# Two attention layers on one core: the softmax sums folded by adding DMAs and summed one block later

## The chip, the core and the metric

The kernel runs on one core of a Trainium2 chip. The metric is the device time of one execution in microseconds (us), as the median of several runs. Engine names are those of the profile: PE is the matmul engine (TensorE) and PEld its weight loads, DVE is VectorE, ACT is ScalarE, POOL is GpSimd, SP is the engine that issues most DMAs. A line such as L431 is line 431 of the kernel before. All arrays are float32.

## What is computed

Two layers, each with its own weights, on x of shape (16, 256, 32, 32), so 16 images of 256 channels and 1024 positions:

```
def layer(x, Wq, bq, Wk, bk, Wv, bv, rel_h, rel_w):      # 4 heads of d = 64 channels
    xf = group_norm(x).reshape(16, 256, 1024)             # 16 groups over the last axis
    q, k, v = (proj(W, b) for W, b in ((Wq, bq), (Wk, bk), (Wv, bv)))   # (16, 4, 64, 1024)
    sim  = einsum('bhdi,bhdj->bhij', q, k)
    qpos = einsum('hdi,bhdj->bhij', (rel_h + rel_w).reshape(4, 64, 1024), q)
    attn = softmax(sim + qpos, axis=-1)
    out  = einsum('bhdn,bhmn->bhdm', v, attn)
    return x + out.reshape(x.shape)
x = layer(x, *layer0); x = layer(x, *layer1)
```

The softmax needs, for each of the 1024 query positions of each head, the sum of 1024 exponentials. How these sums are formed is what the change is about. The kernel takes exp(s - 36) without a maximum, and a flag at the end says whether all sums were in a safe range.

## The kernel before

An image in one layer is a unit; there are 32 units, `u`. A unit has two pairs of heads (`pr`), and a pair of heads is worked in two halves of 512 queries (`half`). So there are 128 blocks, `n`, four to a unit (`b` = 0 to 3). A block with half 0 (n even) and the next one with half 1 (n odd) make a pair of blocks and share one pair of heads.

In a block, the keys come in eight tiles of 128 (`j` = 0 to 7). For each tile DVE first writes the position term into PSUM (`seed`, L338), PE adds q times k onto it (`scores`, L374: 8 instructions, four 64x64 quarters of the array in two passes), ACT takes the exponential into an SBUF tile p (L383), and DVE adds p to a running sum of 128 rows by 2 heads by 512 queries (`add_up` into `acc`, L392 for the first, L394 for the others). Then PE multiplies p by v (`attend`, L408), 128 instructions in two stretches of 64, `values_of_p(0)` and `values_of_p(1)`. Between these, PE already does the scores of tile 0 of the next block.

The partial sum `acc` still has 128 rows, one for each key modulo 128. At the end of an odd block `sums_of_p` (L431) sums the rows of both blocks of the pair with 8 products against a column of ones: 128 rows deep, 32 columns wide, 256 queries long, 16 instructions. ACT copies the values and the sums out of PSUM (`take_out`, L443 in an even block, L448 in an odd one), and SP spreads the sums over partitions into `den_all` (L459, four small DMAs for a pair). In the next block, which is even, `reciprocals` (L467 on DVE, then L470 and L473 on SP) brings 1/sum to all rows as `rden`, and `finish` (L484 and L485 on DVE, 128x1024 each) scales the output and adds bias and x; in layer 1 SP then stores it (L487).

Beside this, each block does two pieces of preparation for what comes next, `first` and `second`: projections of q, k and v (L257, L287) and the position term (L315). Even blocks have two full products there; odd blocks have one full product and the shorter position term. ACT also does the group norm of later units, spread over the blocks: `norm_sums` and `norm_squares` (L182), `norm_apply` (L237). Small products for the mean and the variance (L202, `pm`) stand in the odd blocks, between the two stretches of `values_of_p`.

The order of every engine is the order of the program: the schedule is written by hand, and each engine works off its own list. What couples them:

- Four double banks of PSUM take turns under the names `ring[0]` to `ring[3]`. In a block, the tiles 4 and 6 use the same one (`f1`), so the seed of tile 6 waits until ACT has read the scores of tile 4. Tiles 5, and 0 and 3 of the next block, use `f0`; tile 1 of the next block uses `f1` again, and so does `pm`.
- Scores of a tile come after its seed on DVE and after everything that stands before them on PE. PE does `scores` 1 to 3, `first(0)`, `scores` 4, `second(0)`, `first(1)` and so on.
- A product in two stretches writes the two PSUM banks with exchanged halves of the array. Before the second stretch, POOL sets a one-element `token` when the first is done (`word`, L158), and PE waits for the token. The token is POOL's only work in most blocks; once a unit POOL also takes a power for the norm (L226, L228).

The calls that order DVE's list in `block` before the change:

```
if half == 1: add_up(blocks[n - 1], 7)
seed(blk, 4, f1); add_up(blk, 1)
if half == 0: reciprocals(*before); add_up(blk, 2)
...
add_up(blk, 4); seed(after, 0, f0)
if before: finish(*before)          # even blocks
add_up(blk, 5)
if half == 1: add_up(blk, 6); add_up(blk, 7)
for j in range(1, 4): seed(after, j, ring[j % 3])
if half == 0: add_up(blk, 6)
```

Of the kernel before, what the change touches and what calls it, by code (L numbers as in the profile page):

```python
# [17 lines left out]
P = 128  # L18
# [34 lines left out]
def fast_path(ctx, tc, sh, x, layers, out, W, den_all, token, good, flag):  # L53
# [19 lines left out]

    nc = tc.nc
    B, C, H, N, CC, NT, NH, D, GT = (
        sh.B, sh.C, sh.H, sh.N, sh.CC, sh.NT, sh.NH, sh.D, sh.GT
# [9 lines left out]
    vpool = ctx.enter_context(tc.tile_pool(name="vpool", bufs=2))  # L88
    ppool = ctx.enter_context(tc.tile_pool(name="ppool", bufs=12))
    apool = ctx.enter_context(tc.tile_pool(name="apool", bufs=3))  # L90
    fpool = ctx.enter_context(tc.tile_pool(name="fpool", bufs=2))
    opool = ctx.enter_context(tc.tile_pool(name="opool", bufs=2))
    dpool = ctx.enter_context(tc.tile_pool(name="dpool", bufs=2, space=bass.MemoryType.DRAM))
# [324 lines left out]

    index, rdens = {}, {}

    def sums_of_p(two, po):

        R = P // 4
        for a in range(2):
            for x, blk in enumerate(two):
                for h in range(2):
                    r0 = (2 * x + h) * R  # L430
                    nc.tensor.matmul(  # L431
                        po[r0 : r0 + R, a, QUART:],
                        W.ones[:, :R],
                        accs[blk][:, h, a * QUART : (a + 1) * QUART],
                        start=True, stop=True, tile_position=(0, r0), skip_group_check=True,
                    )

    def take_out(blk, po):

        u, pr, half = blk  # L440
        if half == 0:
            outs[u, pr] = opool.tile([P, 3, HALF], F32, tag="od", name=f"od_{u}_{pr}")
            nc.scalar.copy(  # L443
                outs[u, pr][:, 0, :].rearrange("p (a n) -> p a n", a=2), po[:, :, :QUART]
            )
            return
        od = outs[u, pr]
        nc.scalar.copy(  # L448
            od[:, 1:3, :].rearrange("p z (a n) -> p z a n", a=2),
            po.rearrange("p a (z n) -> p z a n", z=2),  # L450
        )
        keep_sums(od, index[blk] - 1, 2)

    def keep_sums(od, n, count):
        R = P // 4
        for x in range(count):
            for h in range(2):
                r0 = (2 * x + h) * R
                nc.sync.dma_start(  # L459
                    den_all[h * D : (h + 1) * D, n + x, :], od[r0 : r0 + 1, 2, :]  # L460
                )
# [36 lines left out]

    def in_range(den, i):

        t = small.tile([P, den.shape[-1]], F32, tag=f"range{i}", name=f"range{i}")
        nc.vector.tensor_scalar(t, den, DEN_LO, None, ALU.is_ge)
        nc.vector.scalar_tensor_tensor(t, den, DEN_HI, t, ALU.is_le, ALU.mult)
        nc.vector.tensor_reduce(good[:, i : i + 1], t, AX.X, ALU.min)

    def sums_on_rows(acc, pd):

# [55 lines left out]
    def block(n):  # L563
        blk = blocks[n]
        u, b = divmod(n, BPU)
        half = blk[2]
        before = blocks[n - 2][:2] if half == 0 and n > 0 else None
        after = blocks[n + 1] if n + 1 < len(blocks) else None
        one, two = u + 1 < NU, u + 2 < NU

        pieces = u + 1 < NU or b < 2
        if u + 1 == NU and b == 1:
            widen(u, 1)
        f0, f1, f2, f3 = ring
        if not pieces:
            return block_without_pieces(n, half)

        if half == 1:
            add_up(blocks[n - 1], 7)
        for j in range(1, 4):  # L580
            scores(blk, j)
        if b == 3 and u + 3 < NU and units[u + 3][0] not in xt:
            load_x(units[u + 3][0])
        (first, first_out), (second, second_out) = prepare(u, b)
        first(0)
        if b == 0 and one:
            norm_apply(u + 1, range(0, 1))
        if b == 1 and two:
            norm_sums(u + 2, range(9, 11))
        seed(blk, 4, f1)  # L590
        scores(blk, 4)
        add_up(blk, 1)
        if half == 0:
            if before:
                reciprocals(*before)
            add_up(blk, 2)
        if b == 0 and one:
            norm_apply(u + 1, range(1, 5))
        if b == 1 and two:
            norm_sums(u + 2, range(11, 12))  # L600
        if b == 2 and two:
            norm_squares(u + 2, range(0, 5))
        second(0)
        if half == 1:
            second_out()
        first(1)
        first_out()
        seed(blk, 5, f0)
        scores(blk, 5)
        if half == 0:  # L610
            add_up(blk, 3)
            second(1)
            second_out()
        seed(blk, 6, f1)
        scores(blk, 6)
        if half == 0:
            ring[2:] = f3, f2
        seed(blk, 7, ring[2])
        scores(blk, 7)
        if half == 1:  # L620
            add_up(blk, 2)
            add_up(blk, 3)
        add_up(blk, 4)

        if after:
            seed(after, 0, f0)
        if before:
            finish(*before)
        if b == 0 and one:
            norm_apply(u + 1, range(5, 9))  # L630
        if b == 0 and two:
            norm_sums(u + 2, range(0, 2))
        if b == 1 and two:
            norm_sums(u + 2, range(12, G))
        if b == 1 and one:
            norm_apply(u + 1, range(9, 11))
        if b == 2 and two:
            norm_squares(u + 2, range(5, 11))
        po = psum2(ring[3], f"po_{n}")
        values_of_p = attend(blk, po)  # L640
        values_of_p(0)
        if two and half == 1:
            mean, mean_out = (norm_mean if b == 1 else norm_var)(u + 2, zeroed(f1, f"pm_{n}"))
            mean(0)
        if after:
            scores(after, 0)
        if two and half == 1:
            mean(1)
            values_of_p.word()
            mean_out()  # L650
        add_up(blk, 5)
        if half == 1:
            add_up(blk, 6)
            add_up(blk, 7)
        if after:
            for j in range(1, 4):
                seed(after, j, ring[j % 3])
        if half == 0:
            add_up(blk, 6)
        if b == 0 and two:  # L660
            norm_sums(u + 2, range(2, 9))
        if b == 1 and one:
            norm_apply(u + 1, range(11, G))
        if b == 2 and two:
            norm_squares(u + 2, range(11, G))
        values_of_p(1)
        if half == 1:
            sums_of_p(blocks[n - 1 : n + 1], po)
        take_out(blk, po)

    flatden = den_all.rearrange("p n e -> p (n e)")

    def block_without_pieces(n, half):

        blk = blocks[n]
        u, pr, _ = blk
        f0, f1, f2, f3 = ring
        if half == 1:
            add_up(blocks[n - 1], 7)
        for j in range(1, 4):  # L680
            scores(blk, j)
        if half == 1:
            po = pos[n - 1]
            sums_of_p(blocks[n - 1 : n], po)
            nc.scalar.copy(
                outs[u, pr][:D, 2, :].rearrange("p (a n) -> p a n", a=2), po[:D, :, QUART:]
            )
            keep_sums(outs[u, pr], n - 1, 1)
        add_up(blk, 1)
        seed(blk, 7, f2)  # L690
        add_up(blk, 2)
        reciprocals(*(blocks[n - 2][:2] if half == 0 else (u, pr, 1)))
        add_up(blk, 3)
        for j, tag in ((4, f1), (5, f0), (6, f1)):
            scores(blk, j, tag)
        scores(blk, 7)
        add_up(blk, 4)
        if half == 0:
# [11 lines left out]
            seed(blocks[n + 1], 3, f0)  # L710
        add_up(blk, 6)
        if half == 0:
            finish(*blocks[n - 2][:2])
            in_range(flatden[:, : 8 * (n - 2)], 0)
            values_of_p(1)
            take_out(blk, po)
            return
# [8 lines left out]
        pd = psum2(f2, "pd_columns")[:, 0, : 2 * HALF // P]  # L726
        sums_on_columns(acc, pd)
        finish_half(u, pr, 1, po[:, :, :QUART], rden)
        in_range(flatden[:, 8 * (n - 3) : 8 * n], 1)
        in_range(pd, 2)  # L730
        nc.vector.tensor_reduce(good[:, 3:4], good[:, 0:3], AX.X, ALU.min)
        pc = psum2(f1, "pc")[0:1, 0, 0:1]
        nc.tensor.matmul(pc, good[:, 3:4], W.ones[:, 0:1], start=True, stop=True)
# [302 lines left out]
class Weights:  # L1036


    def __init__(self, tc, sh, layers, const):
# [3 lines left out]
        def new(name, shape):  # L1043
            return const.tile(shape, F32, tag=name, name=name)

        self.ident = new("ident", [P, P])
        make_identity(nc, self.ident)
        self.avg, self.ones = new("avg", [P, P]), new("ones", [P, P])
        self.mhalf, self.shift, self.eps = new("mhalf", [P, sh.H]), new("shift", [P, 1]), new("eps", [P, 1])
        for t, v in (  # L1050
            (self.avg, 1.0 / sh.COUNT),
            (self.ones, 1.0),
            (self.mhalf, -0.5),
            (self.shift, -SHIFT),
            (self.eps, EPS),
        ):
            nc.vector.memset(t, v)
        both = range(len(layers))
        self.wq, self.wk, self.wv = (
            [new(f"{n}{l}", [P, sh.CC, sh.C]) for l in both] for n in ("Wq", "Wk", "Wv")  # L1060
# [79 lines left out]
```

## Time and profile before

| | |
|---|---|
| median of 3 runs | 2618.59 us (2617.36 to 2619.73) |
| the profiled execution | 2619.18 us, its span 2617.6 us |
| DVE busy, ACT busy | 92%, 76% of the span |
| seeds, L338 | 1018 of 1229 ns |
| sums over rows, L431 | 1016 instructions, 69.4 us busy, 2% of the chain of waits |
| ACT's copy in odd blocks, L448 | 63 of 1012 ns |
| DMAs issued by POOL | none |
| clock granted to TensorE | 0.997 |

The busy times overlap: quarters of the array work side by side, so instruction durations on PE add up to more than the time that they take. What a stretch of PE's work takes is read from the starts in the timeline. The time line by line is steady: a unit of four blocks takes some 80 us throughout.

### The profile page before, as it was taken

What the parts mean: (1) busy time and instruction counts of PE and PEld (TensorE: products, weight loads), DVE (VectorE), ACT (ScalarE), POOL (GpSimd) and SP (SyncE); (2) the same over time, 40 slices, a digit from 0 to 9 for tenths busy, and PEclk for the clock granted to TensorE, in tenths of its full rate; (3) what the DMA queues carried; (4) which work ended last, traced back from release to release, by engine and by line L of the source; (5) the groups of instructions that cost most, each with busy time, mean ns of one, the idle gap of its engine ahead of it and who ended that gap; (6) DMA issues with size and microseconds to landing.
All of it is one profiled execution on the core that took longest, in us unless ns stands there. A gap on an engine that the chain in (4) does not pass through costs nothing.

```text
span 2617.6 us, 86262 instructions
## 1 busy us (share of the span) xinstructions
PE 2593.7 (99%) x38466; PEld 1404.4 (54%) x38466; DVE 2419.0 (92%) x2200; ACT 1982.8 (76%) x3933; POOL 173.1 (7%) x448
## 2 busy tenths in 40 slices
PE   8999999999999999999999999999999999999998
PEld 4555555555555555555555555555555555555554
DVE  7999999999999999999999999999999999999997
ACT  7778777787777787777877778877778777787653
POOL 1000000000000000000000000000000000000000
PEclk9999999999999999999999999999999999999998
DMA  2000010101101010010100101001010010000010
GB/s 76 19 27 19 18 43 19 35 26 28 34 19 43 19 42 19 19 51 10 42 27 10 50 13 41 27 11 50 19 34 27 16 45 19 19 27 19 26 34 31
DMA packets 61353, 75.21 MB, mean 29 GB/s; under 512 B 42926, under 2 KB 44462, under 8 KB 60974
## 3 DMA queue, kind: packets, MB, share of 16 engines
q1 hardware_dynamic: 60974, 69.63, 9.2%
q8 instruction: 302, 4.95, 0.8%
q14 instruction: 77, 0.63, 0.1%
HBM read 51.78 MB, written 17.30 MB: 26 GB/s over the span
## 4 chain that ended last, share of the span: by engine, by line
PE 97%; DVE 1%; DMA 1%; SPq 0%; issue 0%; ACT 0%; POOL 0%; DVEq 0%
PE ps L374 34%; PE po L408 33%; PE pk L257 8%; PE pq L257 8%; PE pv L287 8%; PE po L431 2%; PE pa L315 2%; PE pm L202 0%; DVE acc L394 0%; DMA den_all<-od 0%; DVE ps L338 0%; SPq L459 0%; DMA x<-in_x_dram 0%; DMA rden<-rd 0%; ACT od L448 0%
## 5 line engine op out<-in xcount | busy, mean ns | idle before, releaser
L383 ACT ACTIVATE p<-ps,shift 128x1024 f32<-128x1024 f32 x1024 | 1091.2, 1114 | 322.6 <-PE ps L374 200.0
L338 DVE TENSOR_TENSOR ps<-abt 128x1024 f32<-128x1024 f32 x1018 | 1221.8, 1229 | 119.6 <-ACT p L383 102.2
L374 PE MATMUL ps<-q,k 64*64 64x512 f32 x8192 | 994.6, 592 | 0.7 <-DVE ps L338 0.7
L394 DVE TENSOR_TENSOR acc<-acc,p 128x1024 f32<-128x1024 f32 x768 | 934.1, 1216 | 18.1 <-ACT p L383 1.4
L408 PE MATMUL po<-p,v 64*64 64x256 f32 x16384 | 933.4, 376 | 0.0
L408 PEld LDWEIGHTS po<-p,v 64*64 64x64 f32 x16384 | 672.2, 133 | 291.2 <-issue 60.2
L374 PEld LDWEIGHTS ps<-q,k 64*64 64x64 f32 x8192 | 305.2, 133 | 416.2 <-issue 286.4
L287 PE MATMUL pv<-Wv,xn 64*64 64x256 f32 x4096 | 244.2, 376 | 0.3 <-DVE var L793 0.3
L257 PE MATMUL pq<-xn,Wq 64*64 64x512 f32 x2048 | 244.0, 592 | 0.2 <-DVE xn L825 0.2
L257 PE MATMUL pk<-xn,Wk 64*64 64x512 f32 x2048 | 242.8, 589 | 0.0
L237 ACT ACTIVATE xn<-x,nshift,rstd 128x128 f32<-128x128 f32 x496 | 211.7, 501 | 0.0
L287 PEld LDWEIGHTS pv<-Wv,xn 64*64 64x64 f32 x4096 | 153.7, 133 | 101.6 <-issue 52.5
L182 ACT ACTIVATE junk<-x,neg 128x128 f32<-128x128 f32 x498 | 195.4, 400 | 0.0
L158 POOL MEMSET token<- 1x1 f32 x380 | 33.5, 88 | 2355.6 <-PE po L408 663.1
L448 ACT COPY od<-po 128x1024 f32<-128x1024 f32 x63 | 63.8, 1012 | 145.3 <-PE po L431 145.3
L392 DVE TENSOR_TENSOR acc<-p,p 128x1024 f32<-128x1024 f32 x128 | 156.0, 1219 | 0.7 <-ACT p L383 0.7
L257 PEld LDWEIGHTS pq<-xn,Wq 64*64 64x64 f32 x2048 | 78.6, 134 | 142.0 <-issue 132.9
L182 ACT ACTIVATE junk<-x 128x128 f32<-128x128 f32 x480 | 145.3, 313 | 0.6 <-DVE x L485 0.6
L257 PEld LDWEIGHTS pk<-xn,Wk 64*64 64x64 f32 x2048 | 75.4, 133 | 123.9 <-issue 123.9
L226 POOL TENSOR_TENSOR rstd<-var,mhalf 128x16 f32<-128x16 f32 x30 | 112.3, 3742 | 59.0 <-ACT var L224 59.0
L297 ACT COPY v<-pv 128x1024 f32<-128x1024 f32 x64 | 64.8, 1012 | 46.5 <-PE pv L287 46.5
L268 ACT ACTIVATE q<-pq,bq 128x1024 f32<-128x1024 f32 x64 | 71.4, 1115 | 33.4 <-PE pq L257 33.4
(72 smaller groups left out, 951.5 us busy)
## 6 DMA issues: line engine op xcount, KB each, us to landing
rden<-rd SPq DMA_DIRECT2D x126, 256.0 KB
x<-in_x_dram SPq DMA_DIRECT2D x32, 512.0 KB
out_dram<-x SPq DMA_DIRECT2D x31, 512.0 KB
den_all<-od SPq DMA_DIRECT2D x254, 2.0 KB
rd<-r SPq DMA_DIRECT2D x127, 4.0 KB
raw<-in_L_conv_Wq_dram SPq DMA_DIRECT2D x2, 256.0 KB
raw<-in_L_conv_Wk_dram SPq DMA_DIRECT2D x2, 256.0 KB
raw<-in_L_conv_Wv_dram SPq DMA_DIRECT2D x2, 256.0 KB
```

Source lines behind the costliest of these rows:

```text
L182: nc.scalar.activation(junk, grouped(xt[units[u][0]], g), func, accum_out=into[:, g : g + 1], **bias)
L226: nc.gpsimd.tensor_tensor(rstd, var, W.mhalf[:, :G], ALU.pow)
L237: nc.scalar.activation(grouped(xns[u], g), grouped(xt[units[u][0]], g), AF.Identity, bias=shift[:, g : g + 1], scale=rstd[:, g : g + 1],)
L257: yield nc.tensor.matmul(pk[c, nh, :], w[l][rs, cc, c0 : c0 + D], xns[u][rs, cc, nh * HALF : (nh + 1) * HALF], start=(t == 0 and cc == 0), ...
L268: nc.scalar.activation(t.rearrange("p (a n) -> p a n", a=NH), pk, AF.Identity, bias=bias[l][:, pr : pr + 1])
L287: yield nc.tensor.matmul(pv[c, a, i, :], xns[u][rs, cc, j0 : j0 + D], W.wv[l][rs, cc, :], start=(t == 0 and cc == 0 and i == 0), stop=(t = ...
L338: nc.vector.tensor_tensor(ps.rearrange("p h (w y) -> p h w y", y=H), ab[:, :, :H].unsqueeze(2).to_broadcast([P, 2, XH, H]), ab[:, :, H + h ...
L374: nc.tensor.matmul(ps[c, h, :], a[hs, j0 : j0 + D], b[hs, columns], start=bool(tag) and i == 0, stop=i == len(terms) - 1, skip_group_check ...
L383: nc.scalar.activation(p, ps, AF.Exp, bias=W.shift)
L392: nc.vector.tensor_tensor(accs[blk], probs[blk, 0], probs[blk, 1], ALU.add)
L394: nc.vector.tensor_tensor(accs[blk], accs[blk], probs[blk, j], ALU.add)
L408: yield nc.tensor.matmul(po[c, a, :QUART], vts[u][rs, j, c0 : c0 + D], p[rs, h, a * QUART : (a + 1) * QUART], start=(t == 0 and j == 0), s ...
```

## The change

The 128 rows of `acc` are first folded by DMAs. `fold` adds rows 64 to 127 onto rows 0 to 63 (an accumulating DMA from POOL's queue, 256 KB). `stack_up` copies rows 0 to 31 of each head into a tile `stack`, which holds both blocks of a pair, 32 rows for each head (two DMAs from SP's queue, 64 KB each). `fold_again` adds rows 32 to 63 onto them (two accumulating DMAs from POOL's queue, 64 KB each). What is left of a pair is one tile of 128 rows by 512, and `sums_of_pair` sums it with four quarter products of 64 rows, 64 columns and 256 queries against a constant `two_ones`. They stand at the end of the next block, which is even, behind `values_of_p(1)`, and write into that block's PSUM tile.

So the sums come out one block later, and what depends on them moves: the copy of the sums, `den_all`, `reciprocals` and `finish` now belong to the odd block after that. Sums 6 and 7 of an odd block are added at the start of the next block. The group norm's work on ACT moves by about a block, and the mean's products from block b = 1 to b = 2. The range check's first part is spread over three late even blocks. The last four blocks keep the old form of the sums.

```
+    def fold(blk):
+        acc = accs[blk]
+        nc.gpsimd.dma_start(acc[:D], acc[D:], accum_op=ALU.add)
+    def stack_up(blk):
+        u, pr, x = blk
+        if x == 0:
+            stacks[u, pr] = spool.tile([P, HALF], F32, tag="stack", name=f"stack_{u}_{pr}")
+        for h in range(2):
+            r0 = x * D + h * R
+            nc.sync.dma_start(stacks[u, pr][r0 : r0 + R, :], accs[blk][:R, h, :])
+    def fold_again(blk):
+        u, pr, x = blk
+        acc = accs.pop(blk)
+        for h in range(2):
+            r0 = x * D + h * R
+            nc.gpsimd.dma_start(
+                stacks[u, pr][r0 : r0 + R, :], acc[R:D, h, :], accum_op=ALU.add
+            )
+    def sums_of_pair(u, pr, po):
+        stack = stacks.pop((u, pr))
+        for x, rs in enumerate(QUARTERS):
+            for c, cs in enumerate(QUARTERS):
+                nc.tensor.matmul(
+                    po[cs, 1 - x, QUART:],
+                    W.two_ones[rs, :],
+                    stack[rs, c * QUART : (c + 1) * QUART],
+                    start=True, stop=True, skip_group_check=True,
+                )
...
-        before = blocks[n - 2][:2] if half == 0 and n > 0 else None
+        before = blocks[n - 3][:2] if half == 1 and n > 2 else None
...
-        if half == 1:
-            add_up(blocks[n - 1], 7)
+        if previous:
+            if half == 0:
+                add_up(previous, 6)
+            add_up(previous, 7)
...
+        first.word()
+        if previous and folded:
+            fold(previous)
+            stack_up(previous)
         first(1)
...
             add_up(blk, 3)
+            second.word()
+            if previous and folded:
+                fold_again(previous)
             second(1)
...
         if before:
             finish(*before)
...
         add_up(blk, 5)
-        if half == 1:
-            add_up(blk, 6)
-            add_up(blk, 7)
         if after:
             for j in range(1, 4):
                 seed(after, j, ring[j % 3])
...
         values_of_p(1)
         if half == 1:
-            sums_of_p(blocks[n - 1 : n + 1], po)
-        take_out(blk, po)
+            if folded:
+                fold_again(previous)
+            take_out(blk, po)
+            pos[n] = po
+            return
+        if n > 1:
+            sums_of_pair(*blocks[n - 2][:2], po)
+        take_out(blk, po, n > 1)
```

## The prediction, made before the changed kernel was run

> **What bounds the kernel now.** I read the page first (busy shares and the chain of waits), then the groups of instructions, then the timeline of one unit.
>
> ```profile
> PE 2593.7 (99%) x38466; PEld 1404.4 (54%) x38466; DVE 2419.0 (92%) x2200; ACT 1982.8 (76%) x3933; POOL 173.1 (7%) x448
> PE 97%; DVE 1%; DMA 1%; SPq 0%; issue 0%; ACT 0%; POOL 0%; DVEq 0%
> ...
> L338 DVE TENSOR_TENSOR ps<-abt 128x1024 f32<-128x1024 f32 x1018 | 1221.8, 1229 | 119.6 <-ACT p L383 102.2
> ```
>
> PE is busy without a break and is the chain of waits. DVE is busy for 92%, and the largest part of its idle time, 102 of some 199 us (2617.6 - 2419.0), is a seed waiting for an exponential. So PE bounds, but DVE has only 199/64 = 3.1 us free for each pair of blocks, and where in the pair this lies decides. The timelines of PE and of DVE over a pair (even block b = 2, odd block b = 3; start, duration, then the instruction):
>
> ```profile
> 1042.27 1.04 PE L374 MATMUL ps<-q,k 64*64 64x512 f32 x8
> ...
> 1062.92 1.04 PE L374 MATMUL ps<-q,k 64*64 64x512 f32 x8
> ...
> 1077.05 1.07 PE L431 MATMUL po<-acc,ones 128*32 128x256 f32 x16
> 1078.05 2.81 PE L374 MATMUL ps<-q,k 64*64 64x512 f32 x24
> 1080.68 1.91 PE L287 MATMUL pv<-Wv,xn 64*64 64x256 f32 x32
> 1082.40 1.04 PE L374 MATMUL ps<-q,k 64*64 64x512 f32 x8
> ```
>
> ```profile
> 1051.37 1.22 DVE L484 TENSOR_TENSOR od<-od,rden 128x1024 f32<-128x1024 f32 x1
> 1052.62 1.29 DVE L485 SCALAR_TENSOR_TENSOR x<-od,bv,x 128x1024 f32<-128x1024 f32 x1
> ...
> 1065.17 2.37 DVE L338 TENSOR_TENSOR ps<-abt 128x1024 f32<-128x1024 f32 x2 [0.80 <-ACT p L383]
> 1067.45 3.74 DVE L394 TENSOR_TENSOR acc<-acc,p 128x1024 f32<-128x1024 f32 x3
> 1071.10 1.23 DVE L338 TENSOR_TENSOR ps<-abt 128x1024 f32<-128x1024 f32 x1
> 1072.26 1.21 DVE L394 TENSOR_TENSOR acc<-acc,p 128x1024 f32<-128x1024 f32 x1
> 1072.28 0.07 DVE L194 MEMSET pm<- 128x16 f32 x1
> 1073.50 2.56 DVE L394 TENSOR_TENSOR acc<-acc,p 128x1024 f32<-128x1024 f32 x2
> 1075.98 3.52 DVE L338 TENSOR_TENSOR ps<-abt 128x1024 f32<-128x1024 f32 x3
> 1080.36 1.23 DVE L338 TENSOR_TENSOR ps<-abt 128x1024 f32<-128x1024 f32 x1 [0.86 <-ACT p L383]
> ```
>
> Take the scores of tile 4 as the mark of a block: 1042.27 (even), 1062.92 (odd), 1082.40 (the next even one). The even stretch takes 20.65 us, the odd one 19.48 (in the pair before, 1022.67 to 1042.27, 19.60). The reader is to see DVE's line in the odd stretch. Seed 6 at 1065.17 waits for the exponential of tile 4, because both tiles use one PSUM bank; it starts 2.25 us after the mark. From there to the end of the three seeds at 1079.50 DVE has no gap, and the third of them is just in time for the scores of tile 3 (1078.05 + 2 x 0.86 = 1079.77). Then seed 4 has a gap of 0.86 ahead of it, and its scores begin 0.81 us after it ends (1081.59). In the odd stretch DVE thus has about 1.7 us in hand for seed 4 and 0.3 us for seed 3.
>
> **What the Trainium skill says.** "TensorEngine Tiling (Array Packing)", section Key Properties: changing the tiling mode drains the engine. The trace agrees: around L431 (128 rows by 32 columns between 64x64 quarters) a pair's end costs more than its 1.00 us. "SBUF — State Buffer", section Who interferes with whom: a DVE instruction with two SBUF inputs contends with a GpSimd instruction only if that reads SBUF. No POOL DMA is in this trace, so it shows neither this nor the opposite. For the prices of the new DMAs I use "DMA: Bandwidth & Descriptors", section Anatomy of one DMA: 2.0 us plus bytes/436 GB/s for a DMA from POOL. An accumulating DMA isn't in the trace.
>
> **The change, part by part.**
>
> *PE.* In an even block's end the second stretch of L408 starts 3.46 us before the scores, and three tiles of scores take 2.57: 6.03. At a pair's end without the mean's products (near the end of the run, starts 2560.97, 2564.53, 2565.53, 2568.16) it is 7.19. So the sums cost 1.15 us a pair. The four new products are 8 instructions of the form of L408 (64*64, 64x256), of which 64 take 3.45 us: 0.43 us, with no change of tiling. On PE alone that is 0.72 us a pair, and 62 pairs are changed (sums in blocks 2 to 124): 45 us.
>
> *DVE, odd stretch.* `finish` moves from the even block into the odd one, between the seed of the next block's tile 0 and sum 5. Sums 6 and 7 go behind the three seeds, but stay ahead of seed 4 of the even block, which is where the stretch ends. So from seed 6 to the end of that seed DVE has fifteen instructions instead of thirteen: seeds 6 and 7, 2.28; sums 2 to 4, 3.65; seed 0, 1.16; `finish`, 2.45 (from 1051.37 to the sum behind it, which starts at 1053.82); sum 5, 1.24 (1.13 where no memset stands beside it); three seeds, 3.41; sums 6 and 7, 2.48; seed 4, 1.23. That is 17.9 us (17.8 in b = 1), each from starts in the timeline. With 2.25 ahead and an estimated 0.15 us from the seed to the first product (a weight load takes 133 ns), the odd stretch is 20.2 us in b = 1 and 20.3 in b = 3. Without the sums PE would be there after 19.48 - 1.15 = 18.3, so PE now waits some 2 us for seeds, first for those of tiles 1 to 3 and then for seed 4. Against before: 20.2 - 19.60 = +0.6 and 20.3 - 19.48 = +0.8. DVE can't work ahead, since seed 6 is tied to the exponential of tile 4.
>
> *Even stretch.* DVE loses `finish` here and has time; PE has 0.43 us more. In b = 2 the mean's products come in: 0.24 us (L408's stretches start 4.55 apart with them, 4.31 without). There seed 1 must wait until ACT has read `pm`, about 1.4 us after the scores of the next tile 0. Without sums 6 and 7 to fill the gap, seeds and two sums then make seed 4 of the odd block about 0.3 us late (my sum: seeds from 1056.7, 3.41 + 2.4 + 1.23, against 1063.6). So +0.43 in b = 0 and +1.0 in b = 2.
>
> *ACT.* The copy of 1012 ns changes places with that of 585 ns, and the norm's pieces move. ACT is idle before most exponentials. Three squares (0.39 each) now stand ahead of the exponential of tile 4 in b = 3, where the trace has a gap of 1.18: I take +0.1 in b = 3.
>
> *Reciprocals.* In the four cases that I looked at, L467 could start 3.7 to 4.5 us after ACT's copy ended. In the odd block the copy ends about 1.6 us after the values, so L467 comes 5.3 to 6.1 us after them, while DVE reaches it after about 5: between nothing and 0.45 us is added ahead of seed 6. I take 0.1. From L467 to `finish` there are about 8 us, as now.
>
> *POOL and SP.* The fold is issued behind the first word and waits for sum 7, which stands before seed 4. Behind it on POOL is the second word, wanted by PE at `second(1)`, some 6 us later. `fold_again` waits on POOL until `stack_up` has landed; behind it is the word of the values, wanted 12.9 us after the mark. By the page's price the fold takes 2.6 us for 256 KB, each 64 KB DMA 2.15, and SP's two issues 1.13 (L470 shows 1.13 for two). With an estimated 1 us on POOL for each issue, that leaves the word about 4 us of air and the sums about 7. Bounds: nothing, or more than the air. I take nothing. On SP only `den_all`'s and the output's DMAs stand behind `stack_up`, many us later.
>
> *The end.* In block 126 the first range check, 3.05 us on DVE, goes from a place where PE waited 4.29 us for a sum. I take -3 us; the longer last check gives 0.2 back.
>
> *Sum.* A unit: 0.43 + 0.6 + 1.0 + 0.9 + 2 x 0.1 = 3.1 us on 80.4. Over 31 units that is 96 us; the mean's work is missing in the last two units (-3), and the end gives 3. So +90 us on the profiled execution's own 2619.2 (span 2617.6 and 1.6 around it): 2709. The median of the runs is 0.6 lower. I put it at **2706 us**.
>
> **The rivals.**
>
> *A, PE stays the bound (faster).* If DVE kept pace, PE's 45 us and the end's 3 would be gained: 2571. Place: seed 4 of the even block. It decides there: DVE's 17.9 us behind seed 6 would have to be under 18.3 - 2.25 - 0.15 = 15.9. For it: DVE's work in a whole pair, 37.8 us, fits into PE's 39.4. Against it: the tie of seed 6 to tile 4, and DVE without a gap for thirteen instructions already.
>
> *B, POOL's queue is late (slower still).* If fold and stack together pass some 11 us, or an issue holds POOL for several us, the values' word comes late in every even block: each us over costs 62 us. With one, 2768. For it: no DMA of this kind is in the trace, and POOL waits at the head of its list. Against: 4 us of air at the page's prices.
>
> *C, the loss is half as large or cancels.* If PE's gain were kept in b = 1 and lost in b = 3, say: 2600 to 2655. Against: all odd blocks have the same list on DVE.
>
> That the quarter products take longer than counted I exclude: they have the form and the bank order of the stretch ahead of them.
>
> **How the numbers follow.** Forecast 0.76, A 0.10, B 0.10, C 0.04. The forecast's own bounds: no weight-load lead, no wait for the reciprocal and no lateness in b = 2 give about 2680; 0.45 us for the reciprocal in each odd block gives 2728, and DVE slowed by POOL's issues some 15 more. The range is 2655 to 2750, with A and most of B outside. What a measurement can tell from no change is about 0.2%. Faster: A and a little of C, 0.11; same 0.02; slower 0.87.
>
> **What would show it.** Right: L431's group at 24 instructions and a new 64*64 group about 0.43 us a pair; odd stretches of 20 to 20.5 us and even ones of 21 to 21.7; L374's products waiting for L338, in the even blocks above all, 1 to 2 us a pair; DVE's idle time moved into the even blocks, and `finish` right behind seed 0 in the odd ones. Wrong: odd stretches of about 18.3 us (A); PE waiting for the token, or for the stack's DMA (B); a gap on DVE between seed 6 and the next seed 4.

## The result, and the profile after

The changed kernel takes 2847.19 us (median of 4 runs, 2840.23 to 2848.94) against 2618.16 us for the kernel before, measured beside it: a ratio of 1.0869, 95% interval 1.0850 to 1.0888. The direction was predicted. The size was not: 229 us were lost where 88 were forecast, and the time lies above the range. Line numbers from here on are those of the changed kernel, which stand 5 higher at the seeds (L343), scores (L379) and values (L413); `finish` is L536 and L537, the reciprocals L519 to L525. In the three kernels below that start from the kernel before, seeds, scores and values have their old numbers or one more.

The page of the changed kernel: span, busy times, the chain of waits by engine, then groups (count, busy time, mean ns, idle time before them and who ended most of it), and last the DMA issues, with the us to landing at the end of a line.

```profile
span 2845.8 us, 86631 instructions
...
PE 2642.4 (93%) x37970; PEld 1468.8 (52%) x37970; DVE 2427.1 (85%) x2200; ACT 1980.7 (70%) x3934; POOL 476.0 (17%) x825
...
PE 45%; DVE 26%; DMA 16%; issue 6%; SPq 4%; ACT 4%; DVEq 0%; POOL 0%; POOLq 0%
...
L343 DVE TENSOR_TENSOR ps<-abt 128x1024 f32<-128x1024 f32 x1018 | 1223.4, 1227 | 335.3 <-ACT neg L217 118.6
...
L448 POOL DMA_DIRECT2D stack<-acc x248 | 198.2, 926 | 258.3 <-DMA stack<-acc 246.3
...
acc<-acc POOLq DMA_DIRECT2D x124, 256.0 KB, 3.5
...
stack<-acc POOLq DMA_DIRECT2D x248, 64.0 KB, 2.6
```

PE was 97% of the chain and is 45%. DVE's work is what it was (2427 us busy, 2419 before), but it now idles 335 us ahead of seeds, 120 before. And DMAs, 1% of the chain before, are 16%: by line `rden` and rd with 7% each and `den_all` with 2%, which the kernel before has too. The last lines are the new DMAs, which no trace had shown. None of them is named in the chain; but they make rd slower, as will be seen.

The stretches between the scores of tile 4 of successive blocks, read from the starts on PE over 31 units, say where the time went. "Predicted" is the mean before plus the prediction's term for that block, with its 0.1 for the reciprocals in the odd ones:

| block | before | predicted | after | after less predicted, times 31 |
|---|---|---|---|---|
| b = 0 | 20.70 | 21.13 | 21.11 | -1 us |
| b = 1 | 19.58 | 20.28 | 20.69 | +13 us |
| b = 2 | 20.66 | 21.66 | 21.60 | -2 us |
| b = 3 | 19.49 | 20.49 | 24.50 | +124 us |

That is 134 of the 141 us that were not foreseen, nearly all of it in b = 3, where the stretches with a variance product lie between 23.1 and 27.35 us. An odd stretch of the b = 1 kind looks as forecast (timeline, PE, from one mark to the next):

```profile
1028.84 1.05 PE L379 MATMUL ps<-q,k 64*64 64x512 f32 x8
...
1043.64 3.36 PE L379 MATMUL ps<-q,k 64*64 64x512 f32 x24 [0.64 <-DVE ps L343]
...
1049.44 1.09 PE L379 MATMUL ps<-q,k 64*64 64x512 f32 x8 [0.72 <-DVE ps L343]
```

20.60 us, and PE waits first for the seeds of tiles 1 to 3 and then for seed 4. The stretch behind block 1, which has no sums to divide by yet and so no `finish`, takes 18.27 us, and the prediction put PE's own bound at 18.3. Now the b = 3 that follows in the same unit:

```profile
1070.04 0.91 SPq L106 DMA_DIRECT2D x<-in_x_dram  x2
...
1072.05 0.24 DVE L519 RECIPROCAL r<-den_all 128x16 f32<-128x16 f32 x1
...
1072.32 1.24 SPq L522 DMA_DIRECT2D rd<-r  x2
...
1075.80 1.23 DVE L343 TENSOR_TENSOR ps<-abt 128x1024 f32<-128x1024 f32 x1 [1.20 <-ACT abt L331]
...
1078.62 1.15 SPq L525 DMA_DIRECT2D rden<-rd  x2
...
1083.58 1.23 DVE L536 TENSOR_TENSOR od<-od,rden 128x1024 f32<-128x1024 f32 x1 [1.75 <-DMA rden<-rd]
...
1086.13 0.07 DVE L199 MEMSET pm<- 128x16 f32 x1
...
1086.35 0.29 PE L207 MATMUL pm<-sum,avg 64*64 64x16 f32 x2 [4.71 <-DVE pm L199]
...
1088.30 4.79 PE L413 MATMUL po<-p,v 64*64 64x256 f32 x64
...
1089.90 3.53 DVE L343 TENSOR_TENSOR ps<-abt 128x1024 f32<-128x1024 f32 x3 [2.58 <-ACT var L229]
```

Read it backwards from the 4.71 us. PE's next instruction is the small variance product, which writes into `pm`. DVE must first set `pm` to zero, in 0.07 us, but this memset stands behind `finish` on DVE's list, and `finish` waits for `rden`. PE works its list in order, so the scores of the next tile 0 and half of the values stand behind that wait. Then the three seeds wait 2.58 us for ACT, which can only now read `pm`. Even DVE's first gap is new: seed 7 waits 1.20 us for ACT's copy, which stands behind four squares. The windows view of the same stretch (window, length, busy time of PE, PEld, DVE, ACT and POOL, then the granted clock, DMA share and GB/s):

```profile
1078.00:1086.30 8.30, 3.63 (x68) 2.29 (x60) 6.44 (x8) 2.86 (x8) 0.09 (x1) 0.85 0.33 80
1086.30:1093.00 6.70, 6.65 (x84) 4.55 (x88) 4.12 (x4) 1.28 (x2) 3.14 (x2) 0.68 0.20 81
...
1083.80:1090.60 6.80, 4.25 (x40) 2.73 (x44) 4.18 (x5) 1.28 (x2) 0.74 (x2) 0.50 0.20 80
```

The wait costs twice: PE gets half of its clock for 6.8 us, which begin during the wait and end 4.3 us behind it (0.68 as a mean of the window behind it), and the 64 products of the values take 4.79 us where the first stretch in this block took 3.63. Over the whole run the clock is 0.981, 0.997 before. The waits of the changed kernel (engine and line, released by whom: us, times, longest):

```profile
PEld ps L379 <- DVE ps L343: 268.9, 355, 2.2
...
PE pm L207 <- DVE pm L199: 105.5, 30, 5.3
...
DVE ps L343 <- ACT var L229: 64.7, 30, 2.6
...
DVE ps L343 <- ACT abt L331: 37.0, 31, 1.2
DVE od L536 <- DMA rden<-rd: 33.8, 44, 2.4
...
PEld po L413 <- POOL token L163: 20.6, 68, 0.8
```

The memset's wait comes 30 times, once in each b = 3 that has the variance. The values wait for POOL's token for 20.6 us (22.6 before): POOL's queue, rival B, is not what delays them.

The trace also gives DVE's account in these 30 stretches. From seed 6 to the end of the next seed 4 its list keeps it busy for 18.0 us as a mean (17.9 counted), but it idles 3.98 us on the way: 2.16 until ACT has read `pm`, 1.21 for ACT's copy and 0.60 for `rden`. A gap there was the last sign that the prediction gave of being wrong.

From this, three suspects for b = 3: the memset behind `finish`; rd's way behind the load of x, which is issued ahead of it on SP (1070.04); and ACT's four squares ahead of the copy. The rival theory is that `finish` on DVE's odd list accounts for the loss by itself and that these waits only take up slack. In the expectations below, theory L says that the cost lies in DVE's list and in what stands behind it (L' counts these waits too), and theory D that it lies in the new DMAs.

### The profile page after: what moved, and what is told of

It reads as the page before. It is cut to its first block, busy times and chain, and to the rows that moved or that the text cites. A ratio compares the mean times of both kernels' runs of the same rounds, so it can differ in the third digit from the quotient of the medians.

```text
span 2845.8 us, 86631 instructions
## 1 busy us (share of the span) xinstructions
PE 2642.4 (93%) x37970; PEld 1468.8 (52%) x37970; DVE 2427.1 (85%) x2200; ACT 1980.7 (70%) x3934; POOL 476.0 (17%) x825
## 4 chain that ended last, share of the span: by engine, by line
PE 45%; DVE 26%; DMA 16%; issue 6%; SPq 4%; ACT 4%; DVEq 0%; POOL 0%; POOLq 0%
PE po L413 16%; PE ps L379 14%; DVE ps L343 13%; DMA rden<-rd 7%; DVE acc L399 7%; DMA rd<-r 7%; PE pq L262 6%; PE pk L262 4%; PE pv L292 3%; DVE x L537 3%; DVE od L536 3%; DMA den_all<-od 2%; SPq L485 2%; ACT od L478 1%; SPq L525 1%
## 5 line engine op out<-in xcount | busy, mean ns | idle before, releaser
L343 DVE TENSOR_TENSOR ps<-abt 128x1024 f32<-128x1024 f32 x1018 | 1223.4, 1227 | 335.3 <-ACT neg L217 118.6
L379 PE MATMUL ps<-q,k 64*64 64x512 f32 x8192 | 1041.4, 604 | 78.1 <-DVE ps L343 71.0
L413 PE MATMUL po<-p,v 64*64 64x256 f32 x16384 | 962.2, 384 | 0.0
L399 DVE TENSOR_TENSOR acc<-acc,p 128x1024 f32<-128x1024 f32 x768 | 938.1, 1222 | 19.1 <-ACT p L388 0.5
L413 PEld LDWEIGHTS po<-p,v 64*64 64x64 f32 x16384 | 704.5, 136 | 289.1 <-issue 60.0
L379 PEld LDWEIGHTS ps<-q,k 64*64 64x64 f32 x8192 | 314.7, 134 | 523.6 <-DVE ps L343 268.9
L448 POOL DMA_DIRECT2D stack<-acc x248 | 198.2, 926 | 258.3 <-DMA stack<-acc 246.3
L292 PEld LDWEIGHTS pv<-Wv,xn 64*64 64x64 f32 x4096 | 174.5, 133 | 80.8 <-issue 47.5
L231 POOL TENSOR_TENSOR rstd<-var,mhalf 128x16 f32<-128x16 f32 x30 | 118.9, 3963 | 78.7 <-ACT var L229 78.7
L207 PE MATMUL pm<-sum,avg 64*64 64x16 f32 x240 | 20.1, 233 | 105.5 <-DVE pm L199 105.5
L432 POOL DMA_DIRECT2D acc<-acc x124 | 100.0, 806 | 60.6 <-DVE ps L343 20.9
```

Of the source, the lines that this page charges most:

```text
L231: nc.gpsimd.tensor_tensor(rstd, var, W.mhalf[:, :G], ALU.pow)
L292: yield nc.tensor.matmul(pv[c, a, i, :], xns[u][rs, cc, j0 : j0 + D], W.wv[l][rs, cc, :], start=(t == 0 and cc == 0 and i == 0), stop=(t = ...
L343: nc.vector.tensor_tensor(ps.rearrange("p h (w y) -> p h w y", y=H), ab[:, :, :H].unsqueeze(2).to_broadcast([P, 2, XH, H]), ab[:, :, H + h ...
L379: nc.tensor.matmul(ps[c, h, :], a[hs, j0 : j0 + D], b[hs, columns], start=bool(tag) and i == 0, stop=i == len(terms) - 1, skip_group_check ...
L399: nc.vector.tensor_tensor(accs[blk], accs[blk], probs[blk, j], ALU.add)
L413: yield nc.tensor.matmul(po[c, a, :QUART], vts[u][rs, j, c0 : c0 + D], p[rs, h, a * QUART : (a + 1) * QUART], start=(t == 0 and j == 0), s ...
```

## Experiments

**The memset ahead of `finish`.** The same instruction, elsewhere on DVE's list.

```diff
+        pm = zeroed(f1, f"pm_{n}") if two and b >= 2 else None
         if before:
             finish(*before)
...
-            mean, mean_out = (norm_mean if b == 2 else norm_var)(u + 2, zeroed(f1, f"pm_{n}"))
+            mean, mean_out = (norm_mean if b == 2 else norm_var)(u + 2, pm)
```

> The changed kernel, with the memset of pm put ahead of finish on DVE. Theory L (DVE's list): in b = 3 the memset stands behind finish, and PE's in-order list waits for it at the mean's products; finish itself stays where it is, so seed 4 of the next block is still late by the fifteen instructions, by seed 7 behind the copy of the position term (1.2 us) and by the wait for rden. Odd stretches of b = 3 fall from 24.5 us to about 22.3, those of b = 1 stay at 20.7; time 2847 - 30 x 2.2 = 2781 us (2750 to 2800). Theory D (the new DMAs are the cost): the memset is no bound of its own, 2840 to 2850 us. If the memset alone were the whole of the unforeseen loss, b = 3 would fall to 20.4 us and the time to 2725.

Measured: 2764.1 us, ratio to the kernel before 1.0555 (1.0525 to 1.0586). The clock is back at 0.999, and b = 3 falls from 24.50 to 21.95 us while the other three stretches stay within 0.14. DVE's idle time in b = 3 falls from 3.98 to 1.72 us, and its wait for ACT to read `pm` is gone. PE's wait in the waits view:

```profile
PE pm L207 <- DVE pm L199: 10.9, 30, 0.4
```

105.5 us of waiting became 10.9. One instruction of 0.07 us, placed behind a wait, was worth 83 us; of these at most 0.018 x 2846 = 51 us are the clock itself.

**`finish` back in an even block, one block later than in the change** (called e3 further below). The folding, the products of a pair and all else of the change stay. (For two pairs of blocks whose image is normed again at once, and in the last blocks, `finish` stays in the odd block.)

```diff
-        if before:
+        if before and not late(n - 3):
             finish(*before)
+        if half == 0 and n > 3 and late(n - 4):
+            finish(*blocks[n - 4][:2])
```

> The changed kernel, with finish put off by one more block: in the even block behind the odd one, where the kernel before has it (but for two pairs whose images are normed again at once, and the last pairs). Sums, folds, reciprocals and all DMAs stay as changed. Theory L: the odd list has thirteen instructions again and neither rden nor finish stands ahead of the memset. b = 1 falls to PE's own 18.3 us, b = 3 to 19.5 to 20.5, even stretches stay at 21.1 and 21.6; time about 2847 - 30 x 6.7 = 2645 us (2620 to 2670). Theory D: the DMAs are all still there, so at least half of the loss stays, 2730 us or more.

Measured: 2655.55 us, ratio 1.0141 (1.0111 to 1.0170); stretches 21.13, 18.42, 21.55, 20.61. With thirteen instructions on DVE's odd list b = 1 drops to PE's bound: the median is 18.27. b = 3 ends a little above the 19.5 to 20.5 expected, for a reason that the timeline shows (DVE, then PE):

```profile
1011.41 3.53 DVE L343 TENSOR_TENSOR ps<-abt 128x1024 f32<-128x1024 f32 x3 [1.59 <-ACT var L229]
...
1018.51 1.09 PE L379 MATMUL ps<-q,k 64*64 64x512 f32 x8 [0.69 <-DVE ps L343]
```

Seeds 1 to 3 use the bank of `pm` first. Sums 6 and 7, which stood ahead of them before, are now behind them, so DVE idles for 1.59 us and seed 4 is late. ACT's copy behind the squares holds seed 7 for 1.21 us as in the change. Together the four stretches are 1.3 us longer than before; in the change they are 7.5 us longer.

**The DMAs alone, added to the kernel before.** POOL and SP do the whole folding in the same places of the program, into tiles of their own whose contents are not used; sums, reciprocals and `finish` are as before.

```diff
+        first.word()
+        if previous and folded:
+            fold(previous)
+            stack_up(previous)
         first(1)
...
+            second.word()
+            if previous and folded:
+                fold_again(previous)
             second(1)
```

> The kernel before, unchanged in its sums and its order on DVE, PE and ACT, with the new DMAs added at the places where the changed kernel has them (the 256 KB fold and the two 64 KB additions from POOL, the two 64 KB copies from SP, for every block but the last four); their result is not used. Theory L: they are hidden, 2618 to 2640 us. Theory D: POOL's tokens or rd and rden come late, 2720 us or more.

A miss for both theories: 2674.01 us, ratio 1.0211 (1.0180 to 1.0243), 56 us where L had expected little and D more. Two waits grew, for `rden` from 0.9 us to 81.4 and for the values' token from 22.6 to 67.9:

```profile
DVE od L507 <- DMA rden<-rd: 81.4, 62, 2.2
...
PEld po L409 <- POOL token L159: 67.9, 68, 5.2
```

The timeline of an even block, SP's queue ahead of POOL and PE:

```profile
1025.41 1.15 SPq L496 DMA_DIRECT2D rden<-rd  x2
1026.66 1.21 SPq L434 DMA_DIRECT2D stack<-folded  x2
...
1030.90 1.69 POOL L440 DMA_DIRECT2D stack<-folded  x2 [9.41 <-DMA stack<-folded]
1032.31 0.30 POOL L159 MEMSET token<- 1x1 f32 x1
1032.67 3.68 PE L409 MATMUL po<-p,v 64*64 64x256 f32 x64 [0.84 <-POOL token L159]
```

In the kernel before the reciprocals belong to even blocks, and their `rden` issue on SP waits for rd's landing. The stack's copies stand behind it, `fold_again` on POOL behind the stack, and the token behind that. rd is slower too: from its issue to that of `rden` 4.4 us pass as a mean, 3.06 in the kernel before, and nothing but the new DMAs was added. Which of the two waits made the 56 us the run doesn't tell. So this run does not price the DMAs as the change has them. The change puts the reciprocals into odd blocks, where `fold_again` stands behind all of the words, and there the token's wait is the 20.6 us shown above. It does show that rival B is real one step of order away.

**Moving `finish` alone, in the kernel before** (called b2 below). No folding and no other moves; `finish` is done in the odd block after its reciprocals, by whose time `rden` has long landed.

```diff
-        if before:
+        if before and not late(n - 2):
             finish(*before)
+        if half == 1 and n > 2 and late(n - 3):
+            finish(*blocks[n - 3][:2])
```

> The kernel before with one thing moved: finish goes from the even block behind a pair into the odd block after it, to the place where the changed kernel has it (behind the seed of the next block's tile 0). Sums, reciprocals and DMAs stay; no DMA is added. Theory L with the memset's wait: the odd lists have fifteen instructions, and in b = 1 and b = 3 PE waits for the memset behind finish, about 2.3 us each: 2618 + 60 x 2.3 = 2756 us (2720 to 2800). Theory L as the prediction counted it, without the memset: +0.8 us an odd block, 2618 + 60 x 0.8 = 2666 us. Theory D: no DMA is new, 2610 to 2630 us.

The direction came as expected, the size did not: 2854.89 us, ratio 1.0902 (1.0870 to 1.0934), 99 us more than expected. Moving two instructions of DVE costs at least as much as the whole change. Both odd stretches are long, 23.30 and 23.44 us, for both hold a mean or variance product here. Its timeline, and the windows around it (length, busy time of PE, PEld, DVE, ACT and POOL, clock, DMA share, GB/s):

```profile
1036.17 1.28 DVE L485 SCALAR_TENSOR_TENSOR x<-od,bv,x 128x1024 f32<-128x1024 f32 x1
1037.47 0.07 DVE L194 MEMSET pm<- 128x16 f32 x1
1037.68 0.23 PE L202 MATMUL pm<-red,avg 64*64 64x16 f32 x2 [2.43 <-DVE pm L194]
1039.01 5.04 PE L408 MATMUL po<-p,v 64*64 64x256 f32 x64
```

```profile
1035.30:1037.70 2.40, 0.01 (x2) 0.04 (x2) 2.37 (x4) 0.09 (x1) 0.00 (x0) 1.00 0.00 0
...
1038.40:1041.80 3.40, 3.40 (x38) 2.58 (x34) 3.26 (x4) 2.46 (x6) 0.00 (x0) 0.51 0.00 0
1041.80:1050.00 8.20, 8.20 (x107) 3.90 (x103) 5.36 (x6) 4.81 (x6) 0.09 (x1) 1.00 0.03 3
```

There is no wait for `rden` in front of `finish` here. Its 2.5 us of work ahead of the memset make PE wait 2.43 us, and soon after the wait the clock is half for 3.4 us. The figures of 0.91 and 0.92 in the next expectation are this half, averaged over windows of 10 us. Over the run the clock is 0.965. How much of the loss is the memset and how much the longer list is left to the next run.

**The same with the memset ahead.**

```diff
+        pm = zeroed(f1, f"pm_{n}") if two and half == 1 else None
-        if before:
+        if before and not late(n - 2):
             finish(*before)
```

> The kernel before with finish in the odd block, as in b2, and the memset of pm ahead of it. Theory L': PE's wait of 2.4 us at the mean's products goes, and with it the lower clock behind it (0.91 to 0.92 over some 20 us in b2). What stays is the list of fifteen instructions: odd stretches of 20.2 to 20.5 us, as the prediction had them, and 2618 + 60 x 0.8 = 2666 us (2655 to 2690). If the clock or the wait have another cause, 2780 us or more.

Measured: 2744.43 us, ratio 1.0481 (1.0460 to 1.0502), clock 0.998. The wait and the lost clock are gone as expected, and they were 110 us. But the rest is 126 us, not the 48 expected, so the time is a miss; the odd stretches are 21.54 and 21.66. The timeline:

```profile
1000.24 4.82 DVE L338 TENSOR_TENSOR ps<-abt 128x1024 f32<-128x1024 f32 x4
...
1001.52 3.36 PE L374 MATMUL ps<-q,k 64*64 64x512 f32 x24
1004.70 1.90 PE L257 MATMUL pq<-xn,Wq 64*64 64x512 f32 x16
1006.42 1.04 PE L374 MATMUL ps<-q,k 64*64 64x512 f32 x8
```

In this order sums 6 and 7 still stand ahead of the three seeds. So the instruction that decides is the fourteenth, seed 3, not seed 4, and behind the scores of tile 3 PE has a full projection to do before those of tile 4: seed 3's scores come after 2.25 + 16.6 + 0.2 = 19.05 us, then 0.86 and 1.72 us of PE, 21.6. That the change puts both sums behind the seeds is worth about 1.3 us in each odd block by this reckoning (21.6 against 20.3), which the expectation had left out. No run moves the two sums alone.

**The load of x moved to b = 0**, behind that block's stack, so that rd has SP's queue to itself.

```diff
-        if b == 3 and u + 3 < NU and units[u + 3][0] not in xt:
-            load_x(units[u + 3][0])
...
+        if b == 0 and two and units[u + 2][0] not in xt:
+            load_x(units[u + 2][0])
```

> The changed kernel, with the load of the next image (two DMAs of 512 KB on SP's queue) moved from the start of b = 3 to b = 0 of the next unit, behind that block's stack_up. Theory L': in b = 3 the small DMA rd queues behind this load, so rden and with it finish come late in the 13 units that load there (their odd stretches are 25.7 us on average, against 23.9 in the others). These fall to about 23.9: 2847 - 13 x 1.8 = 2824 us (2815 to 2835), with no stretch of b = 3 over 25.4. Rival: rd is late because of the folds, which run beside it in every odd block; then the load makes no difference, 2840 to 2850 us.

Measured: 2826.87 us, ratio 1.0799 (1.0777 to 1.0820): 20 us less than the change. b = 3 is 23.85, its longest stretch 25.46 instead of 27.35, and the wait for `rden` falls from 33.8 to 17.9 us.

The rival theory is not refuted by this; both hold in part. From the issue of rd to that of `rden` the change takes 5.8 us as a mean in the 13 blocks with the load. In the other odd blocks it takes 4.2, and so it does in all of them here. But in the kernel before it was 3.06. The fold is issued beside rd (1029.73 and 1029.66 us in the change), and the run with the DMAs alone, where nothing else was added, has 4.4. So with the folding DMAs `rden` is issued about 1.1 us later in every odd block, with or without the load.

**ACT's four squares moved from ahead of `second(0)` to the end of `second`.**

```diff
-        if b == 3 and two:
-            norm_squares(u + 2, range(9, 13))
...
         if half == 1:
             second_out()
+        if b == 3 and two:
+            norm_squares(u + 2, range(9, 13))
```

> The changed kernel, with four squares of the norm in b = 3 put behind ACT's copy of the position term instead of ahead of it. Theory L': seed 7 takes over the PSUM bank of the position term and waits 1.2 us for that copy; without the squares ahead of it DVE's odd list starts 1.2 us earlier in b = 3: 2847 - 30 x 1.2 = 2811 us where finish isn't waiting for rden, less where it is: 2811 to 2840. Rival (ACT isn't on the way): 2845 us or more.

A miss, on the side of the rival: 2857.89 us, ratio 1.0917 (1.0895 to 1.0939), 11 us slower than the change; b = 3 is 24.98. Its waits:

```profile
PE pm L207 <- DVE pm L199: 124.1, 30, 6.2
DVE od L536 <- DMA rden<-rd: 64.8, 57, 3.7
```

Seed 7 no longer waits, but DVE's gain ends in front of `finish`: the wait for `rden` grows from 33.8 to 64.8 us, since rd comes no sooner. PE arrives at the variance product earlier and waits longer, and the clock falls to 0.966. So a stall can hide another, and to take it away alone gains nothing. The clock falls by 0.015 for only 19 us more of waiting because half clock comes in whole stretches: 25 of the 30 waits here are followed by 6.8 us of it, 8 of the 30 in the change, where 15 are followed by 3.4 us and 7 by none.

**All three undone together** (memset ahead, load in b = 0, squares behind).

> The changed kernel with three things put right together: the memset ahead of finish, the squares behind the copy, the load in b = 0. What is left in the odd stretch is the list of fifteen instructions alone. If the prediction's own working was right up to what it overlooked, all odd stretches of b = 3 come to 20.4 to 20.9 us, and the time to 2847 - 30 x 3.8 = about 2730 us (2715 to 2745). If something further is missing, 2760 us or more.

Measured: 2744.22 us, ratio 1.0483 (1.0462 to 1.0504); stretches 21.13, 20.69, 21.60, 21.16. The time is at the upper edge of what was expected, and b = 3 lies above the 20.4 to 20.9. Load and squares together are worth 0.79 us in b = 3, once the memset is out of the way; they were not run apart in that setting. b = 3 is 0.67 above the prediction's 20.49, and DVE still waits for `rden` 45.0 us, 60 times, 0.75 each. In b = 3 this wait, 0.97 us as a mean, is all that DVE idles between seed 6 and the next seed 4; its list takes 17.85 us there (17.9 counted).

**The folding with DVE's load evened out.** `finish` in the even block, the squares behind, and in blocks with a mean or variance some sums ahead of the three seeds, to fill DVE's wait for `pm`: first sums 6 and 7 (6 alone in b = 2), then sum 6 alone everywhere. The diff is that of the first version (f2 below).

```diff
+        if mean_in(n):
+            add_up(blk, 6)
+            if half == 1:
+                add_up(blk, 7)
         if after:
             for j in range(1, 4):
                 seed(after, j, ring[j % 3])
```

> The changed kernel with finish in the even block (as in e3), the squares behind the copy, and sums 6 (and 7, in b = 3) ahead of the three seeds in the blocks that hold the mean's products, so that DVE works while ACT reads pm. Theory L': no list is longer than PE's work; b = 3 falls from 20.6 to about 18.7 us and b = 2 from 21.6 to 21.4; 2655 - 30 x 2.1 = 2592 us (2580 to 2610), faster than before by 0.4 to 1.5%. If the new DMAs hold PE anywhere, 2620 us or more.

Measured: 2603.68 us, ratio 0.9946 (0.9929 to 0.9963); stretches 21.08, 18.42, 21.20, 19.35 (18.7 expected for the last).

> As f2, but in b = 3 only sum 6 stands ahead of the three seeds, sum 7 behind them: in f2 the two sums end 0.7 us after ACT has read pm, and the seeds of tiles 2 and 3 keep PE waiting about 0.6 us. Stretches of b = 3 fall from 19.3 to about 18.7 us: 2603.7 - 30 x 0.6 = 2586 us (2580 to 2595). If the wait has another cause, 2600 to 2606 us.

Measured: 2584.11 us, ratio 0.9869 (0.9852 to 0.9885), 1.3% less than the kernel before; stretches 21.08, 18.42, 21.20, 18.73. Its page:

```profile
PE 2556.1 (99%) x37970; PEld 1452.8 (56%) x37970; DVE 2425.8 (94%) x2200; ACT 1975.8 (77%) x3934; POOL 476.3 (18%) x825
...
PE 87%; ACT 6%; DVE 3%; issue 2%; DMA 1%; SPq 0%; POOL 0%; DVEq 0%; ACTq 0%; POOLq 0%
```

The same DMAs and the same products as the changed kernel, and PE is back at 99%. It lies 13 us above the 2571 of rival A, which had PE busy throughout. With one sum ahead of the seeds the gap is filled but for 0.60 us; with two, b = 3 is 0.62 us longer, since seed 3 comes late there, as in the kernel before with `finish` moved and the memset ahead.

## Why the prediction was off

**What held.** The products of a pair cost what was counted: they start at 1024.11 in the timeline of after and the scores behind them at 1024.55, 0.44 us (0.43 counted). PE's bound without `finish` on the odd list is 18.27 (18.3). The even stretches are within 0.06 us, and in b = 2 DVE waits where the prediction said, at seed 1 until ACT has read `pm` (the 118.6 us of the page, 3.95 us each). DVE's list of fifteen instructions is the mechanism in b = 1: 20.69 us as a mean, and 18.42 once `finish` is taken off it. POOL's work stays hidden, and rival B fell in the order that the change has. The prediction also took from "SBUF — State Buffer" (section Who interferes with whom) that DVE with two SBUF inputs contends with a GpSimd instruction only if that reads SBUF; with 124 large accumulating DMAs in the trace, the sums L399 take 1222 ns, 1216 before, and the seeds 1227, 1229 before, so none of it is seen here.

**Which step failed.** The sum has `finish` move on DVE and costs the move by DVE's list alone, up to the next seed 4. It does not ask who waits for what stands behind `finish`: that cost was put at nothing, without a reason. One such instruction is named there, and only as a time: "1.13 where no memset stands beside it". Its reader is PE, in order, in the middle of the values. This is the wait that the run with the memset ahead removes: 2.55 of the 4.01 us in b = 3, 83 us in all with the clock. The clock itself has no term in the sum, since before PE never stood still.

**Two terms that were too small.** "From L467 to `finish` there are about 8 us, as now", with 0.1 us for the reciprocals, was true of the kernel before (8.3 to 8.6 us as means). In b = 1 of the change it is 9.4 us (1029.38 to 1038.76), and `finish` waits 0.36 us; in the b = 3 shown it is 11.5. Two things lengthen it. The load of x, whose place on SP did not change, is now ahead of rd; moving that load gave 20 us. And with the folding DMAs, of which the fold is issued beside rd, `rden` is issued about 1.1 us later behind rd in all odd blocks; the prediction looked for the cost of the new DMAs at the token and the stack, and took nothing. The other small term is "I take +0.1 in b = 3" for ACT: the squares' cost was sought at the exponential of tile 4, which had a gap, while the copy of the position term stands behind them too, and seed 7 waits 1.20 us for it. Load and squares together are the 0.79 us. What then remains, 0.67 us in b = 3 and 0.41 in b = 1, goes with the wait for `rden`, 0.97 and 0.52 us, the only idle time that DVE's list has there in the run with the three undone. That the folding DMAs are its cause is argued from the times of rd; no run of the change takes them away from rd.

The prediction's sum also gives 2708.6 us, not the 2706 that it states; this is small beside the miss.

**The rivals.** A fell for the reason given, and the last experiment shows that it was within reach of an order that keeps DVE's pairs even. C fell as well: b = 1 and b = 3 both lost. B's sign, PE waiting for the token, did not come: 20.6 us, 22.6 before. What no case held was a second loss of the forecast's own kind on top of the first.

## What to carry to other kernels

When a step is moved on an in-order engine, list every instruction that lands behind it, tiny ones above all, and ask for each which engine reads its result and what stands behind that reader. Where a wait is added to a step, do the same for the DMAs that it waits for: what is ahead of them on their queue in the new place. An engine with enough time in a pair of blocks still binds in one of them if its work falls unevenly, and the order within the block decides: here the same work in three orders took 2847, 2604 and 2584 us.

## What the hardware showed that was not expected

Short idle times of PE cost more than themselves, and in whole steps. In all traces of this case the clock is either full or half; but for the end of a run, half comes in stretches of 3.4 us, at times two in a row. "TensorE: Matmul & The Clock Gate" (Part 1) states an idle window of about 3.4 us before the clock is halved. Waits below it count here too: with `finish` moved alone, 56 of the 57 waits for the memset, 2.26 to 2.43 us each, were followed by 3.4 us of half clock; over that run the clock was 0.965. With the memset ahead the waits and these stretches were gone, and the clock was 0.998. In the change, 23 of 30 waits of 2.86 to 5.35 us were followed by half clock. Why a wait of 2.87 us was followed by it in some blocks and not in others, no run settles.

The accumulating DMAs landed later than the prices taken from "DMA: Bandwidth & Descriptors" (Anatomy of one DMA): 3.5 us for 256 KB and 2.6 for 64 KB, 2.6 and 2.15 estimated. POOL was busy 0.81 and 0.93 us for each issue, close to the 1 us estimated, for which the prediction named no source. SP's copies, for which it took the same price of 2.15 us, held the additions behind them for 4.2 us from the first one's issue (1035.26 to 1039.43). A small transfer can wait for a large one: from rd, 4 KB, to the issue behind it 6.3 us passed in the block shown, where the load of x was ahead of it on SP's queue, 4.2 us with the load moved, and 3.06 us in the kernel before, without the folds.
